# Taller edge steps for the last image, a PSUM read moved to ScalarE, and a new dealing-out of the last stages' steps

## The chip, the cores and the metric

The kernel runs on one NeuronCore of a Trainium2 chip. The metric is the device time of one execution in microseconds (us), lower is better. Five engines run in parallel, each with its own queue of instructions in order: TensorE (PE in the profile; its weight loads are PEld), VectorE (DVE), ScalarE (ACT), GpSimd (POOL) and SyncE (SP, which here only issues DMAs). They wait for each other through semaphores. ScalarE issues DMAs too, and those issues stand in the same queue as its computations.

## The reference, cut to what matters

Everything is float32. Layer 0 is an attention layer with linear attention over 64x64 pixels and 512 channels for 4 images; it ends in `y = BN(conv1x1(out)) + x`. Layer 1 works on that y, and most of the change lies in it:

```python
sobel = jnp.sqrt(sobel_h ** 2 + sobel_v ** 2 + 1e-08)      # four 3x3 edge filters, per channel
lap   = jnp.abs(dwconv(x, K_LAP))
diag  = jnp.maximum(jnp.abs(dwconv(x, K_D1)), jnp.abs(dwconv(x, K_D2)))
grad  = jnp.sqrt(sobel ** 2 + lap ** 2 + 1e-08)
E = jnp.stack([sobel, lap, diag, grad])
y = jnp.einsum('kbchw,koc->kbohw', E, w_branch) + ...       # 4 branches, 512 -> 128 channels each
feat = jax.nn.gelu(y, approximate=False)
pooled = ef.mean(axis=(2, 3))                               # over the whole image
att = sigmoid(gelu(pooled @ w_att1.T + b) @ w_att2.T + b)   # one factor per channel
z = jnp.einsum('bchw,oc->bohw', ef * att, w_fuse) + b_fuse  # then layer norm over channels, gelu, + x
```

The mean over the image stands between the branches and the fusion: no pixel of an image can be fused before all its edges have been computed.

## The kernel before, in words

**Stages.** For each image the *front* (class `Group`, four groups of heads per image, lines 220 to 610) computes the attention. Three generators then carry an image to the end: `project_out` (y, 32 steps, each one `yps` bank of 16 matmul records and one VectorE pass), `edge_branches` (the edges) and `fuse_out` (attention factors, then the fusion `zps` and the layer norm). While the front of image b runs, `advance` deals out steps of the three generators of image b-1 by planned lengths, so the edges of images 0, 1 and 2 run amid front work on every engine. This part covers about 1200 to 4340 us for the edges. After the front of the last image only generators are left (from about 4340 us): the rest of image 2 and all of image 3.

**Edges (lines 667 to 757).** A step u covers 4 rows of the image. `edges(u, pair)` loads a window of 6 rows of two of the four channel chunks and makes four maps of them: 11 VectorE operations (lines 696 to 722) and 4 ScalarE operations (Square L709, Abs L713, Square L719, Sqrt L723). `branches(u, ks, maps)` then multiplies two of the four branches, 256 pixels each, into the two halves of one PSUM bank (tile `br`, L730), applies the gelu to each half on ScalarE (L737, with a running sum for the mean) and stores both (L742). Each of images 0 to 2 has 16 steps u and thus 32 calls of `branches`, 96 in all; the last image has 32 more. One fp32 product of the code is two records in the profile, so that a call is 8 products and 16 records on TensorE.

**Order.** `manual_schedule` keeps TensorE's instructions in the order in which the code states them. For the other engines a scheduler sets the order when the program is built. Semaphore waits are derived from the tiles that instructions share. PSUM tiles of tag `ps` (`br`, `zps`, `yps`, `proj` and others) rotate over four banks.

**ScalarE's queue in the front.** After each projection (`project`, L262) ScalarE copies the bank (L268), for queries also applies a relu (L273), and issues four DMAs (L277). The gelu of a `branches` call stands behind whatever of this came first, and behind a table load when the function set changes (Sqrt and Gelu need different tables).

**The end of the program (lines 930 to 960).** After half of the last image's `project_out` steps, each of the 64 steps of the last image's edges is followed by exactly one step of `rest`: the 16 remaining `project_out` steps, then image 2's `fuse_out`. What is left of them, and the last image's `fuse_out`, comes last. In `fuse_out`, ScalarE squares each `zps` bank (L810) and VectorE reads the same bank once more to make z (L812).

Of the kernel before, what the change touches and what calls it, by code (L numbers as in the profile page):

```python
# [8 lines left out]
F32 = mybir.dt.float32  # L9
AF = mybir.ActivationFunctionType  # L10
ALU = mybir.AluOpType
AX = mybir.AxisListType

B, C, H, W = 4, 512, 64, 64
N = H * W
P = 128
NCH = C // P
NG = 4
NJ = N // 512
WB = W + 2  # L20
# [45 lines left out]
SHARE_Y, SHARE_E, SHARE_F = 90.0, 450.0, 100.0  # L66

WAIT_Y, WAIT_E, WAIT_F = 32.0, 16.0, 26.0

LEFT_E = 14.0  # L70

# [12 lines left out]
def conv_seq_kernel(  # L84
    ctx: ExitStack, tc, x, wqkv, dpk, wtab, proj, projc, pwk, bn0, consts, vec, watt1, batt1, watt2, wbr, wfuse, out
):
    nc = tc.nc

    const = ctx.enter_context(tc.tile_pool(name="const", bufs=1))
    small = ctx.enter_context(tc.tile_pool(name="small", bufs=2))  # L90
# [15 lines left out]
    def ps_tile(name):  # L106
        return psum.tile([P, 512], F32, tag="ps", name=name)
# [8 lines left out]
    def rows(ap, width=W):  # L116
        return ap.rearrange("p (r c) -> p r c", c=width)
# [55 lines left out]
    fbias = const.tile([P, 4], F32, name="fbias")  # L173
# [43 lines left out]
    first = ExitStack()  # L217
# [449 lines left out]
    def edge_branches(b, efs, pool_sb, side):  # L667

        y = ys[b % 2]
        with ExitStack() as stack:  # L670
            pool = stack.enter_context(tc.tile_pool(name=f"E{b}", bufs=2, side=side, reuse_waits="tile"))
            wbr_sb = pool.tile([P, 4, NCH, P], F32, name="wbr_sb", bufs=1)
            nc.sync.dma_start(out=wbr_sb, in_=wbr)
            share = SHARE_E / (2 * NJ * 4)

            slot = (2, 0, 1, 3)
            run = WB * 4 - 2
            yield 0.0

            def edges(u, pair):  # L680

                win = pool.tile([P, 2, 6 * WB], F32, name="win", tag="win")
                nc.sync.dma_start(
                    out=win,
                    in_=y[2 * pair : 2 * pair + 2].rearrange("c p r w -> p c (r w)")[:, :, 4 * u * WB : (4 * u + 6) * WB],
                )
                above, mid, below = (win[:, :, n * WB : (n + 4) * WB] for n in range(3))
                maps = pool.tile([P, 4, 2, 4 * WB], F32, name="maps", tag="maps", bufs=3)
                flat = maps.rearrange("p k c x -> p (k c x)")
                lap, sobel, grad = (maps[:, n, :, 0:run] for n in (0, 2, 3))  # L690


                dv = pool.tile([P, 2, 2, 4 * WB], F32, name="dv", tag="dv", bufs=1)
                down, smooth = dv[:, 0], dv[:, 1]
                dvs = dv.rearrange("p k c x -> p (k c x)")
                nc.vector.tensor_sub(down, below, above)
                nc.vector.tensor_add(smooth, below, above)
                nc.vector.scalar_tensor_tensor(smooth, mid, 2.0, smooth, ALU.mult, ALU.add)

                half = 2 * 4 * WB
                nc.vector.tensor_sub(flat[:, half : 3 * half - 2], dvs[:, 2 : 2 * half], dvs[:, 0 : 2 * half - 2])  # L703

                nc.vector.tensor_add(lap, mid[:, :, 0:run], mid[:, :, 2 : run + 2])
                nc.vector.scalar_tensor_tensor(lap, mid[:, :, 1 : run + 1], -6.0, lap, ALU.mult, ALU.add)
                nc.vector.tensor_add(lap, lap, smooth[:, :, 1 : run + 1])
                lap2 = pool.tile([P, 2, run], F32, name="lap2", tag="lap2", bufs=1)
                nc.scalar.activation(lap2, lap, AF.Square)  # L709
                first, second = (  # L710
                    maps[:, n : n + 2].rearrange("p k c x -> p (k c) x")[:, :, 0:run] for n in (0, 2)
                )
                nc.scalar.activation(first, first, AF.Abs)  # L713


                sv = flat[:, 3 * half : 4 * half - 2]
                nc.vector.tensor_add(sv, dvs[:, 0 : half - 2], dvs[:, 2:half])
                nc.vector.scalar_tensor_tensor(sv, dvs[:, 1 : half - 1], 2.0, sv, ALU.mult, ALU.add)
                nc.scalar.activation(second, second, AF.Square)  # L719
                nc.vector.tensor_add(sobel, sobel, grad)  # L720

                nc.vector.scalar_tensor_tensor(grad, lap2, SOBEL_EPS, sobel, ALU.add, ALU.add)
                nc.scalar.activation(second, second, AF.Sqrt, bias=sobel_eps)  # L723
                return maps

            def branches(u, ks, maps):
                ps = ps_tile("br")
                for n, k in enumerate(ks):
                    for c in range(NCH):
                        nc.tensor.matmul(  # L730
                            rows(ps)[:, 4 * n : 4 * n + 4, :], lhsT=wbr_sb[:, k, c, :],
                            rhs=rows(maps[c // 2][:, slot[k], c % 2, :], WB)[:, :, 0:W],
                            start=(c == 0), stop=(c == NCH - 1),
                        )
                o = pool.tile([P, 2, 256], F32, name="ef_o", tag="ef_o")
                for n, k in enumerate(ks):
                    nc.scalar.activation(  # L737
                        o[:, n, :], ps[:, 256 * n : 256 * n + 256], AF.Gelu,
                        bias=shift1[:, k : k + 1], scale=scale1[:, k : k + 1], accum_out=pool_sb[:, k, u : u + 1],
                    )  # L740
                step = ks[1] - ks[0]
                nc.scalar.dma_start(  # L742
                    out=efs[u // 2][:, ks[0] : ks[1] + 1 : step, 256 * (u % 2) : 256 * (u % 2) + 256], in_=o
                )

            held = []
            for u in range(2 * NJ + 1):
                first = [edges(u, 0)] if u < 2 * NJ else []
                yield share if u else share + WAIT_E
                if held:  # L750
                    branches(u - 1, (1, 2), held)
                    yield share
                    branches(u - 1, (0, 3), held)
                    yield share
                if first:
                    held = first + [edges(u, 1)]
                    yield share if u else share + WAIT_E

    def fuse_out(b, efs, pool_sb, side):

        y = ys[b % 2]
        with ExitStack() as stack:
            pool = stack.enter_context(tc.tile_pool(name=f"F{b}", bufs=2, side=side, reuse_waits="tile"))
# [39 lines left out]
            share = SHARE_F / (NJ * 5)  # L803

            def fuse(c, ef, zs, total):
                ps = ps_tile("zps")
                for k in range(4):
                    nc.tensor.matmul(ps, lhsT=wf_sb[:, k, ts(c, P)], rhs=ef[k], start=(k == 0), stop=(k == 3))  # L808
                sq = total if c == 0 else pool.tile([P, 512], F32, name="sq", tag="sq", bufs=3)
                nc.scalar.activation(sq, ps, AF.Square, bias=fbias[:, c : c + 1])  # L810
                z = pool.tile([P, 512], F32, name="z", tag="z", bufs=6)
                nc.vector.tensor_scalar(z, ps, fbias[:, c : c + 1], None, ALU.add)  # L812
                zs.append(z)
                if c:
                    nc.gpsimd.tensor_add(total, total, sq)
# [46 lines left out]
    def stages(b, heads, cheads, folded, side="right"):  # L862

        efs = [dram.tile([P, 4, 512], F32, name=f"ef{j}") for j in range(NJ)]
        pool_sb = small.tile([P, 4, 2 * NJ], F32, name="pool_sb")
        return [
            project_out(b, heads, cheads, folded, side), edge_branches(b, efs, pool_sb, side),
            fuse_out(b, efs, pool_sb, side),
        ]
# [9 lines left out]
    behind, due = [], [0.0]  # L879
# [58 lines left out]


    projected, edged, fused = stages(last.b, last.heads, last.cheads, last.folded, "left")  # L940
    next(fused)
    next(edged)
    next(projected)
    while len(behind) > 1:
# [2 lines left out]
    next(behind[0])  # L947
    for _ in range(NCH * NJ // 2):
        next(projected)
    rest = [projected] + behind  # L950
    for n, _ in enumerate(edged):
        while rest and next(rest[0], None) is None:
            rest.pop(0)
    for stage in rest + [fused]:
        for _ in stage:
            pass

# [94 lines left out]
```

## Time and profile before

| | |
|---|---|
| median of 3 runs (range) | 5078.56 us (5077.92 to 5086.61) |
| the profiled execution's own time | 5063.71 us |
| span of its instructions | 5061.9 us |
| mean granted TensorE clock | 0.967 |
| 4340 to 4600 us: PE / DVE / ACT busy | 254.2 / 97.8 / 57.6 of 260 us |
| 4597 to 4907 us: PE / DVE / ACT / POOL busy | 233.8 / 276.7 / 229.9 / 94.9 of 310 us |
| 4910 to 5062 us: PE / DVE / ACT busy | 121.4 / 80.4 / 71.0 of 152 us |
| table loads of ScalarE from 4440 us on | 78, of 1283 ns each |

The profile lists an engine's busy time and, in its views of waits and groups, the idle time before an instruction with what ended it. "issue" means that nothing visible ended it. `ACTq` and `SPq` rows are DMA issues: the engine's sequencer is occupied, though the engine doesn't count as busy. The end of a matmul record is modelled: records that follow each other without a wait overlap slightly in the listing.

### The profile page before, as it was taken

The page shows a single profiled execution, that of the slowest core. Times are in us where ns is not written, and L with a number is a line of the kernel's source. Part 1 is how long each engine was busy: PE and PEld are TensorE (multiplying, and loading weights), DVE is VectorE, ACT ScalarE, POOL GpSimd, SP SyncE. Part 2 cuts the span into 40 slices and gives each one's busy share as a digit, 9 for nine tenths or more (in the row PEclk, how much of TensorE's full clock was granted, in tenths as well). Part 3 has the DMA queues.
Part 4 walks back from the last instruction along what each step waited for, and adds up shares of the span by engine and source line. Part 5 has one row for each costly group of instructions (what it writes and reads, how often), then busy time and mean ns, then how long its engine had stood idle before and what let it go on. Part 6 is the DMA issues. An engine that isn't in the chain of part 4 may idle for free. (4 is left out here: it accounts for less than half of the span.)

```text
span 5061.9 us, 107134 instructions
## 1 busy us (share of the span) xinstructions
PE 4702.0 (93%) x46362; PEld 2739.7 (54%) x46362; DVE 2124.7 (42%) x2960; ACT 1626.5 (32%) x2833; POOL 392.7 (8%) x291
## 2 busy tenths in 40 slices
PE   9999999999999999799899999899989898898777
PEld 5665654455666554454465655454456665445443
DVE  1222221116556433211455653431146557157965
ACT  2112111004444423200345442320024445035765
POOL 0000000000000013100000000310000000001335
PEclk9999999999999999899999999999999999999889
DMA  6444466666656565676555665657655553774425
GB/s 196 138 123 130 132 206 190 158 165 181 192 189 183 179 205 170 197 178 156 176 176 181 193 202 176 213 188 167 163 173 175 184 169 129 200 184 118 151 88 172
DMA packets 635945, 866.26 MB, mean 171 GB/s; under 512 B 324393, under 2 KB 395081, under 8 KB 617041
## 3 DMA queue, kind: packets, MB, share of 16 engines
q1 hardware_dynamic: 551504, 758.68, 51.8%
q10 hardware_dynamic: 83968, 100.74, 6.4%
q8 instruction: 364, 5.96, 0.5%
q14 instruction: 109, 0.88, 0.1%
HBM read 578.09 MB, written 213.98 MB: 156 GB/s over the span
## 5 line engine op out<-in xcount | busy, mean ns | idle before, releaser
L262 PE MATMUL proj<-xt,w_sb 128*128 128x512 f32 x2048 | 955.8, 610 | 52.9 <-DMA xt<-in_x 31.8
L655 PE MATMUL yps<-hd,fold_sb 128*128 128x512 f32 x2048 | 899.6, 596 | 9.7 <-DMA hd<-heads 8.7
L396 PE MATMUL cv<-inp,mat 32*32 32x512 f32 x20480 | 730.2, 597 | 35.4 <-issue 27.3
L262 PEld LDWEIGHTS proj<-xt,w_sb 128*128 128x128 f32 x2048 | 382.7, 194 | 523.3 <-issue 450.7
L655 PEld LDWEIGHTS yps<-hd,fold_sb 128*128 128x128 f32 x2048 | 384.9, 190 | 493.5 <-issue 445.3
L396 PEld LDWEIGHTS cv<-inp,mat 32*32 32x32 f32 x20480 | 420.3, 103 | 314.6 <-issue 154.2
L730 PE MATMUL br<-maps,wbr_sb 128*128 128x256 f32 x2048 | 495.0, 396 | 51.8 <-ACT maps L713 42.2
L808 PE MATMUL zps<-ef,wf_sb 128*128 128x512 f32 x1024 | 469.9, 610 | 53.5 <-DMA ef<-ef 19.0
L730 PEld LDWEIGHTS br<-maps,wbr_sb 128*128 128x128 f32 x2048 | 399.7, 198 | 165.9 <-issue 51.3
L284 PEld LDWEIGHTS val<-w_sb,xt 128*128 128x128 f32 x4096 | 470.2, 192 | 33.9 <-issue 26.1
L284 PE MATMUL val<-w_sb,xt 128*128 128x128 f32 x4096 | 484.9, 277 | 0.6 <-DVE vt L291 0.3
L660 DVE SCALAR_TENSOR_TENSOR yt<-yps,shift,xr 128x512 f32<-128x512 f32 x128 | 96.1, 750 | 871.8 <-PE yps L655 788.9
L268 ACT COPY strip<-proj 128x512 f32<-128x512 f32 x256 | 149.1, 582 | 928.5 <-PE proj L262 910.4
L451 PE MATMUL corr<-near,ckt 128*32 128x160 f32 x8192 | 333.6, 315 | 35.0 <-DMA near<-near 28.4
L808 PEld LDWEIGHTS zps<-ef,wf_sb 128*128 128x128 f32 x1024 | 196.1, 195 | 296.6 <-issue 235.6
L241 POOL TENSOR_TENSOR mat<-dp_sb 128x1280 f32<-128x1280 f32 x32 | 77.2, 2414 | 3464.5 <-PE cv L396 2951.0
L451 PEld LDWEIGHTS corr<-near,ckt 128*32 128x32 f32 x8192 | 256.9, 111 | 131.5 <-issue 73.1
L703 DVE TENSOR_TENSOR maps<-dv 128x1054 f32<-128x1054 f32 x128 | 162.6, 1271 | 366.9 <-PE br L730 366.9
L312 ACT ACTIVATE kt<-tr 128x512 f32<-128x512 f32 x128 | 75.8, 593 | 528.9 <-PE tr L310 345.9
L737 ACT ACTIVATE ef_o<-br,shift,scale 128x256 f32<-128x256 f32 x256 | 142.3, 559 | 283.5 <-PE br L730 251.9
L360 DVE RECIPROCAL rec<-rec 128x512 f32<-128x512 f32 x64 | 214.4, 3350 | 1.7
L812 DVE TENSOR_SCALAR z<-zps,fbias 128x512 f32<-128x512 f32 x128 | 94.9, 744 | 283.4 <-DMA out<-z 97.0
(125 smaller groups left out, 4135.7 us busy)
## 6 DMA issues: line engine op xcount, KB each, us to landing
xt<-in_x SPq DMA_DIRECT2D x316, 512.0 KB
near<-near SPq DMA_DIRECT2D x512, 264.0 KB
inp<-strip ACTq DMA_DIRECT2D x1024, 64.0 KB
win<-y SPq DMA_DIRECT2D x128, 396.0 KB
near<-vt SPq DMA_DIRECT2D x512, 66.0 KB
y<-yt SPq DMA_DIRECT2D x128, 264.0 KB
yr<-y SPq DMA_DIRECT2D x128, 264.0 KB
heads<-q SPq DMA_DIRECT2D x128, 256.0 KB
```

What stands on the lines that cost most here:

```text
L262: nc.tensor.matmul(ps, lhsT=self.w[t][:, c, :], rhs=xs[self.b, j][c], start=(c == 0), stop=(c == NCH - 1))
L268: nc.scalar.copy(s, ps)
L284: nc.tensor.matmul(ps[:, ts(c, P)], lhsT=xs[self.b, j][n][:, ts(c, P)], rhs=self.w[VALUE][:, n, :], start=(n == 0), stop=(n == NCH - 1),)
L360: nc.vector.reciprocal(rec, rec)
L396: nc.tensor.matmul(rows(banks[i])[32 * j : 32 * j + 32, :, c0:c1], lhsT=self.mat[t][q, j, (dx + 2) * 8 + 4 * b : (dx + 2) * 8 + 4 * b + 4, :],
L451: nc.tensor.matmul(self.banks[jj][32 * i : 32 * i + 32, 160 * b : 160 * b + 160], lhsT=self.held["c", i][:, at : at + 32], rhs=v[:, 4 * n ...
L655: nc.tensor.matmul(ps, lhsT=fold_sb[g // NG][:, g % NG, ts(c, P)], rhs=hd[g], start=(g == 0), stop=(g == 2 * NG - 1),)
L660: nc.vector.scalar_tensor_tensor(yt[:, :, 1 : W + 1], rows(ps), shift0[:, c : c + 1], rows(xr), ALU.add, ALU.add)
L703: nc.vector.tensor_sub(flat[:, half : 3 * half - 2], dvs[:, 2 : 2 * half], dvs[:, 0 : 2 * half - 2])
L730: nc.tensor.matmul(rows(ps)[:, 4 * n : 4 * n + 4, :], lhsT=wbr_sb[:, k, c, :], rhs=rows(maps[c // 2][:, slot[k], c % 2, :], WB)[:, :, 0:W] ...
L737: nc.scalar.activation(o[:, n, :], ps[:, 256 * n : 256 * n + 256], AF.Gelu, bias=shift1[:, k : k + 1], scale=scale1[:, k : k + 1], accum_o ...
L808: nc.tensor.matmul(ps, lhsT=wf_sb[:, k, ts(c, P)], rhs=ef[k], start=(k == 0), stop=(k == 3))
```

## The change

Four things change.

1. The edges of the last image (`side == "left"`) go in steps of 8 rows instead of 4: half as many instructions, each twice as long, and each branch fills a bank of its own (512 pixels).
2. For that, `branches` is rewritten for all images: a bank is taken when the next one is needed, and each branch's gelu now stands directly behind its own matmuls, ahead of the second branch's matmuls. For images 0 to 2 the two branches still share a bank.
3. In image 2's fusion, z is made by ScalarE (Identity with bias) instead of VectorE.
4. The steps of `rest` are dealt out by planned lengths (5.5 us for a step of `project_out`, 2.9 for one of `fuse_out`) against the planned length of the edges; three shares are kept for the steps that make the attention factors; the last `fuse_out` takes its memory and loads its weights when `project_out` has ended, not before; the edges' memory is given back at the very end.

```diff
-            share = SHARE_E / (2 * NJ * 4)
+            tall = 8 if side == "left" else 4
+            steps, wide = H // tall, tall * W
+            share = SHARE_E / (steps * 4)
...
             def branches(u, ks, maps):
-                ps = ps_tile("br")
+                o = pool.tile([P, 2, wide], F32, name="ef_o", tag="ef_o")
                 for n, k in enumerate(ks):
+                    if n * wide % 512 == 0:
+                        bank = ps_tile("br")
+                    ps = bank[:, n * wide % 512 : n * wide % 512 + wide]
                     for c in range(NCH):
                         nc.tensor.matmul(
-                            rows(ps)[:, 4 * n : 4 * n + 4, :], lhsT=wbr_sb[:, k, c, :],
+                            rows(ps), lhsT=wbr_sb[:, k, c, :],
                             rhs=rows(maps[c // 2][:, slot[k], c % 2, :], WB)[:, :, 0:W],
                             start=(c == 0), stop=(c == NCH - 1),
                         )
-                o = pool.tile([P, 2, 256], F32, name="ef_o", tag="ef_o")
-                for n, k in enumerate(ks):
                     nc.scalar.activation(
-                        o[:, n, :], ps[:, 256 * n : 256 * n + 256], AF.Gelu,
+                        o[:, n, :], ps, AF.Gelu,
                         bias=shift1[:, k : k + 1], scale=scale1[:, k : k + 1], accum_out=pool_sb[:, k, u : u + 1],
                     )
...
-                nc.vector.tensor_scalar(z, ps, fbias[:, c : c + 1], None, ALU.add)
+                if b == B - 2:
+                    nc.scalar.activation(z, ps, AF.Identity, bias=fbias[:, c : c + 1])
+                else:
+                    nc.vector.tensor_scalar(z, ps, fbias[:, c : c + 1], None, ALU.add)
...
-    rest = [projected] + behind
-    for n, _ in enumerate(edged):
-        while rest and next(rest[0], None) is None:
-            rest.pop(0)
-    for stage in rest + [fused]:
+    rest, spent, given = [projected] + behind, 0.0, 0.0
+    def fill():
+        nonlocal spent
+        while rest and spent < given:
+            spent += FILL_Y if rest[0] is projected else FILL_F
+            if next(rest[0], None) is None:
+                if rest.pop(0) is projected:
+                    next(fused)
+    for share in edged:
+        if not share:
+            break
+        given += share * REST / SHARE_E
+        fill()
+    for _ in range(3):
+        next(fused)
+        given += (16 * FILL_Y + 44 * FILL_F - REST) / 3
+        fill()
+    for stage in rest + [fused, edged]:
```

More of the change, by code (lines that the diff above doesn't have):

```diff
@@ L68 @@
 WAIT_Y, WAIT_E, WAIT_F = 32.0, 16.0, 26.0
+FILL_Y, FILL_F = 5.5, 2.9
+REST = 16 * FILL_Y + 40 * FILL_F
 LEFT_E = 14.0
@@ L673, in edge_branches @@
             nc.sync.dma_start(out=wbr_sb, in_=wbr)
-            share = SHARE_E / (2 * NJ * 4)
+            tall = 8 if side == "left" else 4
+            steps, wide = H // tall, tall * W
+            share = SHARE_E / (steps * 4)
             slot = (2, 0, 1, 3)
-            run = WB * 4 - 2
+            run = WB * tall - 2
             yield 0.0
             def edges(u, pair):
-                win = pool.tile([P, 2, 6 * WB], F32, name="win", tag="win")
+                win = pool.tile([P, 2, (tall + 2) * WB], F32, name="win", tag="win")
                 nc.sync.dma_start(
                     out=win,
-                    in_=y[2 * pair : 2 * pair + 2].rearrange("c p r w -> p c (r w)")[:, :, 4 * u * WB : (4 * u + 6) * WB],
-                )
-                above, mid, below = (win[:, :, n * WB : (n + 4) * WB] for n in range(3))
-                maps = pool.tile([P, 4, 2, 4 * WB], F32, name="maps", tag="maps", bufs=3)
+                    in_=y[2 * pair : 2 * pair + 2].rearrange("c p r w -> p c (r w)")[
+                        :, :, tall * u * WB : (tall * u + tall + 2) * WB
+                    ],
+                )
+                above, mid, below = (win[:, :, n * WB : (n + tall) * WB] for n in range(3))
+                maps = pool.tile([P, 4, 2, tall * WB], F32, name="maps", tag="maps", bufs=3)
                 flat = maps.rearrange("p k c x -> p (k c x)")
                 lap, sobel, grad = (maps[:, n, :, 0:run] for n in (0, 2, 3))
-                dv = pool.tile([P, 2, 2, 4 * WB], F32, name="dv", tag="dv", bufs=1)
+                dv = pool.tile([P, 2, 2, tall * WB], F32, name="dv", tag="dv", bufs=1)
                 down, smooth = dv[:, 0], dv[:, 1]
@@ L698, in edges @@
                 nc.vector.scalar_tensor_tensor(smooth, mid, 2.0, smooth, ALU.mult, ALU.add)
-                half = 2 * 4 * WB
+                half = 2 * tall * WB
                 nc.vector.tensor_sub(flat[:, half : 3 * half - 2], dvs[:, 2 : 2 * half], dvs[:, 0 : 2 * half - 2])
@@ L734, in branches @@
                         )
-                o = pool.tile([P, 2, 256], F32, name="ef_o", tag="ef_o")
-                for n, k in enumerate(ks):
                     nc.scalar.activation(
-                        o[:, n, :], ps[:, 256 * n : 256 * n + 256], AF.Gelu,
+                        o[:, n, :], ps, AF.Gelu,
                         bias=shift1[:, k : k + 1], scale=scale1[:, k : k + 1], accum_out=pool_sb[:, k, u : u + 1],
                     )
[L741 to L744, printed above, removed]
+                at, step = wide * u % 512, ks[1] - ks[0]
+                nc.scalar.dma_start(out=efs[wide * u // 512][:, ks[0] : ks[1] + 1 : step, at : at + wide], in_=o)
             held = []
-            for u in range(2 * NJ + 1):
-                first = [edges(u, 0)] if u < 2 * NJ else []
+            for u in range(steps + 1):
+                first = [edges(u, 0)] if u < steps else []
                 yield share if u else share + WAIT_E
@@ L757, in edge_branches @@
                     yield share if u else share + WAIT_E
+            yield 0.0
     def fuse_out(b, efs, pool_sb, side):
@@ L864, in stages @@
         efs = [dram.tile([P, 4, 512], F32, name=f"ef{j}") for j in range(NJ)]
-        pool_sb = small.tile([P, 4, 2 * NJ], F32, name="pool_sb")
+        pool_sb = small.tile([P, 4, 2 * NJ if side == "right" else NJ], F32, name="pool_sb")
         return [
@@ L940, in conv_seq_kernel @@
     projected, edged, fused = stages(last.b, last.heads, last.cheads, last.folded, "left")
-    next(fused)
     next(edged)
```

## The prediction, made before the changed kernel was run

> **What bounds the kernel now.** I read the page's first part, then the busy time by stage, then single calls of `branches` in the timeline, then the groups of the late stage.
>
> ```profile
> PE 4702.0 (93%) x46362; PEld 2739.7 (54%) x46362; DVE 2124.7 (42%) x2960; ACT 1626.5 (32%) x2833; POOL 392.7 (8%) x291
> ```
>
> ```profile
> 1200.00:1790.00 590.00, 562.09 (x6911) 368.69 (x6910) 322.92 (x486) 273.98 (x500) 11.97 (x5) 0.98 0.61 190
> 2490.00:3080.00 590.00, 565.22 (x7178) 377.77 (x7177) 323.52 (x491) 267.08 (x476) 12.46 (x5) 0.98 0.61 191
> 3770.00:4340.00 570.00, 513.13 (x6546) 336.09 (x6542) 327.24 (x484) 255.34 (x445) 7.48 (x7) 0.95 0.54 169
> 4597.00:4907.00 310.00, 233.81 (x679) 141.27 (x679) 276.68 (x328) 229.93 (x317) 94.90 (x56) 0.87 0.40 125
> ```
>
> Columns of the second, after the length of the stretch: busy PE, PEld, DVE, ACT, POOL, then the granted clock. In the three stretches that hold the edges of images 0, 1 and 2, TensorE is busy 1640 of 1750 us: it is the bound, and what stops it costs time. From 4597 to 4907 us, the edges of the last image beside image 2's fusion, VectorE is busy 277 of 310 us, and TensorE waits there: VectorE is the bound. So the change's taller edges, z and dealing-out lie in these 310 us; its rewritten `branches` lies in the 1750 as well.
>
> **What the skill says.** "PSUM — Partial Sum Buffer", section "PSUM bank collisions raise a hardware error": two engines may not touch one bank and quadrant at once, and the scheduler orders them whatever halves they use. The program before never had to, since both branches were multiplied before any gelu; no trace shows it yet. "TensorE: Matmul & The Clock Gate", section "Step-by-step: what each phase is for": matmuls stay in program order, so a waiting one holds all behind it; and its "Part 1: The HAM clock gate": idle TensorE falls to half clock for a window of 3.4 us. The trace agrees on the second:
>
> ```profile
> 3883.40:3886.80 3.40, 0.11 (x4) 0.11 (x4) 3.40 (x2) 1.31 (x2) 0.00 (x0) 0.99 0.65 148
> 3886.80:3890.20 3.40, 3.40 (x45) 1.83 (x46) 3.40 (x7) 1.17 (x1) 0.00 (x0) 0.51 0.17 46
> ```
>
> After a gap of 3.47 us the next 3.4 us ran at 0.51. Of the gaps of 2.5 to 3.5 us in this trace 17 of 18 were followed so, of those of 1.5 to 2.5 us 7 of 19. "SBUF — State Buffer", section "SBUF: two separate sides": VectorE, with two SBUF inputs, and GpSimd share a port pair that one holds at a time. L717 took 0.70 us in a quiet stretch and 872 ns in the mean from 4597 to 4907 us, where GpSimd runs: it agrees.
>
> **Part 1: gelu ahead of the second branch, images 0 to 2.** The order of the built programs shows TensorE's first 22,901 instructions unchanged, but in all 96 calls the first matmul of the second branch now waits for the first branch's gelu. Queued behind it: the rest of the call and every later projection and convolution. The price of one call comes from the timeline:
>
> ```profile
> 1570.33 3.62 PE L730 MATMUL br<-maps,wbr_sb 128*128 128x256 f32 x16
> 1573.88 2.55 PE L451 MATMUL corr<-near,ckt 128*32 128x160 f32 x64
> 1570.53 0.58 ACT L268 COPY strip<-proj 128x512 f32<-128x512 f32 x1 [2.38 <-PE proj L262]
> 1571.15 2.41 ACTq L277 DMA_DIRECT2D inp<-strip  x4
> 1573.59 1.28 ACT L737 ACT_TABLE_LOAD   x1 [2.48 <-issue]
> 1574.89 0.56 ACT L737 ACTIVATE ef_o<-br,shift,scale 128x256 f32<-128x256 f32 x1
> 1575.35 0.20 ACT L737 ACTIVATION_READ_ACCUMULATOR ef_o<-br,shift,scale 128x1 f32 x1
> ```
>
> The eighth of the 16 records ends near 1572.2. The gelu can't start before 1574.89: ScalarE first copies a projection, issues four DMAs, loads a table. It ends, with its accumulator, at 1575.55; a released matmul starts some 0.05 us later (in this trace L713 ended at 4603.08 and L730 started at 4603.13). So TensorE will stand from 1572.2 to 1575.6: 3.4 us, where before it went on. An idle ScalarE would give the least: 0.04 us to start, 0.56, 0.10, 0.05, or 0.75 us.
>
> I did this for all 96 calls, with ScalarE's queue (copies, DMA issues, table loads) as in the trace; the order of ScalarE's instructions around the call is the same in 85 of the 96. Visible gaps: 33 calls at the least 0.75 us, 24.7 us; 13 up to 1.5 us, 12.8; 21 up to 2.5 us, 43.5; 19 up to 4 us, 61.2; 10 above, 51.5. Sum 193.7 us. To it:
>
> - Records without a wait overlap by some 0.17 us in the listing (a group of 16 takes 3.62 us, the next starts 3.45 after it), and a restarted group takes 0.1 us longer (1.13 against 1.03 for four records): 96 x 0.27 = 26 us.
> - Half clock: 29 gaps above 2.5 us at 90% and 21 of 1.5 to 2.5 us at 37%, each losing half of 3.41 us: 44 + 13 = 57 us, of which I take 45, as small matmuls are bound by weight loads too.
> - Given back: TensorE idles 106 us in the three stretches (28, 25 and 53). Gaps within 14 us after a call come to 18 us, within 30 us to 42; a later TensorE finds these waits shorter. I take -30.
>
> Together +235 us. Bounds: from below ScalarE never has a backlog, 96 x (0.75 + 0.27) = 98, less 42 given back, about +55; from above 194 + 26 + 57 - 5, about +270. A gain is excluded, since nothing is removed from TensorE here.
>
> **Part 2: edges of 8 rows.** VectorE: in the quiet timeline a 528-wide operation follows the last after 0.615 us and the 1054-wide L703 takes 1.17 us, so that 526 elements cost about 0.56 us and the fixed part is about 0.05 us. 16 x 11 = 176 instructions go for the whole image; of the 23 steps at work in the 310 us, half, 126 instructions, 6 us. ScalarE: 0.632 us for 524 and 1.07 for 1048 elements leave 0.2 us fixed: 46 instructions fewer in the window, 9 us. The program has 51 loads of tables for Sqrt and Gelu before, 27 after; in the window some 18 x 1.283 = 23 us go. Gelus: 25 pairs of 0.559 become one of 0.77 (estimate from the slope): 9 us. TensorE: 128x256 and 128x512 records go at the same rate (0.215 and 0.43 us), so nothing.
>
> **Part 3: z on ScalarE.** VectorE loses 32 x 0.740 us:
>
> ```profile
> L812 DVE TENSOR_SCALAR z<-zps,fbias 128x512 f32<-128x512 f32 x32 | 23.5, 740 | 12.1 <-ACT total L810 10.5 <-DMA out<-z 1.5
> L810 ACT ACTIVATE sq<-zps,fbias 128x512 f32<-128x512 f32 x24 | 16.1, 675 | 8.2 <-PE zps L808 7.7 <-ACT ef_o L737 0.5
> L730 PE MATMUL br<-maps,wbr_sb 128*128 128x256 f32 x386 | 109.7, 443 | 48.1 <-ACT maps L713 42.2 <-DVE z L812 5.1 <-ACT maps L723 0.7
> ```
>
> ScalarE gains 32 x 0.675 = 22 us (priced as L810, same bank and size). Edge operations and the next gelus queue behind it; TensorE gets each `zps` bank back only after both readings by ScalarE.
>
> **Part 4: dealing out.** 12 four-row calls' worth of branches instead of 9 now come before the last `yps`. That moves 3 x 3.45 = 10 us of matmuls into a stretch where TensorE is full (+10 us), and with them about 3 x 7.3 x 1.27 = 28 us of VectorE and 17 us of ScalarE work out of the 310 us. The order after shows image 2's fusion used up before the last edges, so the attention factors still lie bare; the last step's chain is twice as tall: I take +6 us. The fusion's weights (three DMAs on SP's queue) now queue where `project_out` ends, ahead of later windows; 250 us of edges cover them, about 3 us if not. POOL gets nothing.
>
> Sum for the 310 us: VectorE 277 - 6 - 23 - 28 = 220; ScalarE 230 + 22 - 9 - 23 - 9 - 17 = 194; TensorE 234 - 10 = 224. VectorE's share of the stretch was 277 of 310; with the same looseness 220 becomes 246, a gain of 64. Less 10, 6 and 3: **-45 us**. Bounds: -75 if the stretch closes to its engines; +5 if ScalarE's chains make it looser (1.3 times 220 is 286).
>
> **Sum.** Against the profiled execution, span 5061.9 and time 5063.71 us: +235 - 45 = +190, 5253.7 us. It lies 14.9 us below the median of the runs, 5078.56, to which I add the same: **5268.6 us**.
>
> **The rivals.**
> - *ScalarE without backlog.* TensorE's stops let ScalarE drain, and every call costs the least: 98, no half clock, 20 given back: +78 - 45 = +33, 5111 us. For it: ScalarE is busy only 46% of the stretches. Against: the copies, DMA issues and table load stand directly ahead of the gelu, produced by the projection just before. 13%.
> - *The waits are swallowed.* Faster: the stops take the place of TensorE's idle 106 us, so that the calls cost nearly nothing, and the tail's -45 remains: 5034 us. It decides if a call costs below 0.47 us (45 / 96). Against: only 18 to 42 us of idle lie near the calls. 4%.
> - *ScalarE becomes the late bound.* Part 1 as forecast, no tail gain: 5314 us. 13%.
> - *Forecast.* 70%.
>
> **How the numbers follow.** The measurement tells 0.2%, about 10 us, from no change. The likeliest case gives 5268.6, with part 1 from 180 to 265 and the tail from -65 to -15: 5194 to 5329. The range reaches down towards the first rival, 5150, and up to 5335. Faster 0.04 (swallowed), same 0.03 (between that and the first rival), slower 0.93.
>
> **What would show it.** A wait of TensorE `br` on ScalarE `ef_o`, absent from the groups of before in these stretches, about 96 times and near 190 us; the last edge stretch shortened to about 250 us with VectorE no longer 90% busy; fewer table loads by 24. Wrong if that wait is below 100 us, if clock and projections stay as they were, or if the late stretch doesn't shrink.

## The result and the profile after

The changed kernel takes 5304.25 us (median of 4 runs, 5303.24 to 5309.46) against 5078.24 us before: ratio 1.0441, 95% interval 1.0424 to 1.0457, or +226 us where +190 was forecast. The profiled execution took 5303.73 us with a span of 5301.9, 240 us more than that of before. First part of its page, then its busy time by stretch (length; PE, PEld, DVE, ACT, POOL; clock); the first three stretches run from the first to the last `br` matmul of images 0, 1 and 2, the fourth is B of the table below:

```profile
PE 4769.4 (90%) x46106; PEld 2710.2 (51%) x46106; DVE 2092.2 (39%) x2752; ACT 1604.7 (30%) x2713; POOL 394.5 (7%) x291
```

```profile
1208.90:1868.10 659.20, 567.59 (x6776) 366.00 (x6774) 319.20 (x479) 278.20 (x498) 11.97 (x5) 0.95 0.52 162
2593.20:3266.40 673.20, 577.09 (x7018) 377.13 (x7017) 322.28 (x487) 270.73 (x472) 12.44 (x5) 0.95 0.52 162
3974.40:4607.90 633.50, 532.72 (x6504) 338.46 (x6502) 321.14 (x475) 256.97 (x441) 7.40 (x7) 0.93 0.47 146
4868.52:5144.77 276.25, 222.19 (x481) 94.62 (x479) 215.53 (x145) 184.12 (x215) 92.19 (x54) 0.90 0.41 130
```

The same four stretches before:

```profile
1204.20:1775.90 571.70, 543.79 (x6776) 357.20 (x6774) 318.59 (x479) 271.59 (x494) 11.97 (x5) 0.98 0.60 187
2497.60:3071.40 573.80, 549.01 (x7018) 367.82 (x7017) 321.87 (x487) 263.61 (x468) 12.46 (x5) 0.98 0.60 188
3777.20:4336.20 559.00, 505.91 (x6504) 330.89 (x6502) 323.31 (x477) 252.49 (x439) 7.48 (x7) 0.95 0.53 167
4593.98:4905.14 311.16, 236.54 (x688) 143.63 (x687) 277.60 (x328) 228.73 (x313) 94.90 (x56) 0.87 0.40 125
```

TensorE ran exactly as many records in the first three as before (6776, 7018, 6504) and took longer for them. The lines of the view of waits over these images, costliest first (us in total, times, longest):

```profile
PE br L741 <- ACT ef_o L746: 180.5, 96, 6.4
PE proj L265 <- DMA xt<-in_x: 31.1, 3, 22.4
PE cv L399 <- issue: 28.6, 21, 2.7
```

The first line did not exist before: 96 stops for 96 calls. The others did, at much the same size. The call that the prediction worked out (1570.33 us there) now looks so:

```profile
1637.99 1.89 PE L741 MATMUL br<-maps,wbr_sb 128*128 128x256 f32 x8
1643.25 2.79 PE L741 MATMUL br<-maps,wbr_sb 128*128 128x256 f32 x8 [3.37 <-ACT ef_o L746]
1638.19 0.58 ACT L271 COPY strip<-proj 128x512 f32<-128x512 f32 x1 [2.38 <-PE proj L265]
1638.80 2.42 ACTq L280 DMA_DIRECT2D inp<-strip  x4
1641.25 1.28 ACT L746 ACT_TABLE_LOAD   x1 [2.48 <-issue]
1642.55 0.56 ACT L746 ACTIVATE ef_o<-br,shift,scale 128x256 f32<-128x256 f32 x1
1643.01 0.19 ACT L746 ACTIVATION_READ_ACCUMULATOR ef_o<-br,shift,scale 128x1 f32 x1
```

The 16 records have become 8 and 8, with 3.37 us between them (3.4 was worked out), in which ScalarE does what it did before: copy, four DMA issues, table load, gelu. The second eight take 2.79 us instead of 1.89; the granted clock was 0.66 from 1643.2 to 1646.6 us.

By stretch, in us (length, and in brackets TensorE's idle time and what the clock took, that is the time weighted with the part not granted):

| stretch | before | after | difference |
|---|---|---|---|
| edges of image 0 | 571.7 (27.9; 11.9) | 659.2 (91.6; 32.4) | +87.5 |
| edges of image 1 | 573.8 (24.8; 11.9) | 673.2 (96.1; 34.1) | +99.4 |
| edges of image 2 | 559.0 (53.1; 27.3) | 633.5 (100.8; 46.1) | +74.5 |
| start and the two stretches between | 2631.7 | 2641.9 | +10.2 |
| from there to the last projection (A) | 257.8 | 260.6 | +2.8 |
| to the last edge matmul (B) | 311.2 | 276.2 | -35.0 |
| to the end (C) | 156.8 | 157.2 | +0.4 |

The images' edges lost 261.4 us; the late part (A, B, C) gained 31.8. ScalarE's table loads fell from 211 to 187, by the 24 that the prediction named.

### The profile page after: what moved, and what is told of

Read it like the earlier page. It is cut to its first block, busy times and chain, and to the rows that moved or that the text cites. A ratio compares the mean times of both kernels' runs of the same rounds, so it can differ in the third digit from the quotient of the medians.

```text
span 5301.9 us, 106106 instructions
## 1 busy us (share of the span) xinstructions
PE 4769.4 (90%) x46106; PEld 2710.2 (51%) x46106; DVE 2092.2 (39%) x2752; ACT 1604.7 (30%) x2713; POOL 394.5 (7%) x291
## 5 line engine op out<-in xcount | busy, mean ns | idle before, releaser
L741 PE MATMUL br<-maps,wbr_sb 128*128 128x256 f32 (+1 forms) x1792 | 542.8, 452 | 199.0 <-ACT ef_o L746 181.4
L741 PEld LDWEIGHTS br<-maps,wbr_sb 128*128 128x128 f32 x1792 | 357.3, 207 | 386.5 <-ACT ef_o L746 221.4
L816 PEld LDWEIGHTS zps<-ef,wf_sb 128*128 128x128 f32 x1024 | 196.4, 195 | 305.3 <-issue 246.8
L711 DVE TENSOR_TENSOR maps<-dv 128x1054 f32<-128x1054 f32 (+1 forms) x112 | 159.8, 1427 | 445.0 <-PE br L741 444.9
L746 ACT ACTIVATE ef_o<-br,shift,scale 128x256 f32<-128x256 f32 (+1 forms) x224 | 133.2, 595 | 433.3 <-PE br L741 390.5
L412 ACT ACTIVATE co<-cv 128x256 f32<-128x256 f32 x256 | 93.8, 397 | 339.1 <-PE cv L399 339.1
## 6 DMA issues: line engine op xcount, KB each, us to landing
near<-near SPq DMA_DIRECT2D x512, 264.0 KB
y<-yt SPq DMA_DIRECT2D x128, 264.0 KB
yr<-y SPq DMA_DIRECT2D x128, 264.0 KB
```

The source lines that it names most:

```text
L741: nc.tensor.matmul(rows(ps), lhsT=wbr_sb[:, k, c, :], rhs=rows(maps[c // 2][:, slot[k], c % 2, :], WB)[:, :, 0:W], start=(c == 0), stop=(c ...
L746: nc.scalar.activation(o[:, n, :], ps, AF.Gelu, bias=shift1[:, k : k + 1], scale=scale1[:, k : k + 1], accum_out=pool_sb[:, k, u : u + 1],)
```

## Experiments

Ratios are against the kernel before on the same chip, whose median there was 5051 to 5062 us; lengths of stretches are from each run's profile. The diffs show the lines that matter; `...` stands for what was left out.

**1. The branches mended, all else changed.** Images 0 to 2 only; `parts` holds the `ps` of both branches:

```diff
                     for c in range(NCH):
                         nc.tensor.matmul(...)
+                    if tall == 4:
+                        continue
                     nc.scalar.activation(o[:, n, :], ps, AF.Gelu, ...)
+                for n, k in enumerate(ks):
+                    if tall == 8:
+                        break
+                    nc.scalar.activation(o[:, n, :], parts[n], AF.Gelu, ...)
```

> The changed kernel with one thing undone: for images 0 to 2 both branches are multiplied before either gelu, as in the kernel before; everything for the last images stays changed. Theory (the three image stages lost 261 us to the waits for the first gelu, and the late part alone gained 32): about 5304 - 261 = 5043 us, 0.993 of the kernel before, with no wait of TensorE's second branch on the gelu and granted clock back near 0.967. Rival (the loss comes from how the changed program orders the other engines, or from the late part): stays above 5200 us.

Measured 5025.91 us, ratio 0.9933 (0.9916 to 0.9951). The three stretches take 566.1, 575.1 and 562.8 us, together 1704.0 against 1704.5 before and 1965.9 changed; the wait is gone. All of the loss is in this one ordering, and the rest of the change is a gain of 0.7%, with 1 outside its interval. The longest waits left in these images are of other kinds:

```profile
PE corr L454 <- DMA near<-near: 29.5, 7, 9.2
```

**2. The gelus' new place alone, in the kernel before.**

```diff
                 for n, k in enumerate(ks):
+                    ps = bank[:, 256 * n : 256 * n + 256]
                     for c in range(NCH):
                         nc.tensor.matmul(...)
+                    if side == "right":
+                        nc.scalar.activation(o[:, n, :], ps, AF.Gelu, ...)
                 for n, k in enumerate(ks):
+                    if side == "right":
+                        break
                     nc.scalar.activation(o[:, n, :], bank[:, 256 * n : 256 * n + 256], AF.Gelu, ...)
```

> The kernel before with one thing changed: for images 0 to 2 each gelu stands directly behind its own branch's matmuls, in the shared bank. Theory: 5078 + 261 = about 5339 us, 1.051 of before, with a wait of br on ef_o of about 180 us in 96 places and some 60 us more of lost clock. Rival (the loss needs the other parts of the change): below 5150 us.

Measured 5317.38 us, ratio 1.0503 (1.0476 to 1.0531); the three stretches together 1979.2 us, +274.7. It needs nothing else of the change.

```profile
PE br L732 <- ACT ef_o L738: 181.7, 96, 6.3
PE br L732 <- ACT maps L713: 41.2, 8, 11.4
```

**3. The gelus' new place, but a bank for each branch.**

```diff
-                    if n * wide % 512 == 0:
-                        bank = ps_tile("br")
-                    ps = bank[:, n * wide % 512 : n * wide % 512 + wide]
+                    ps = ps_tile("br")[:, 0:wide]
```

> The changed kernel with the gelus where the change put them, but each branch of images 0 to 2 in a PSUM bank of its own. Theory (the wait comes from the shared bank, not from the place of the gelu): the wait for the same call's gelu is gone; the calls take two of the four rotating banks, so that some calls wait for a gelu of an earlier call; I put these at 10 to 60 us, which gives 5055 to 5105 us. Rival (the place of the gelu in ScalarE's queue costs, whatever the bank): stays within 30 us of 5304.

Measured 5033.78 us, ratio 0.995 (0.9932 to 0.9968); stretches 1707.0 us. Its longest waits in these images are no gelus:

```profile
PE corr L454 <- DMA near<-near: 27.9, 7, 8.8
PE proj L265 <- DMA xt<-in_x: 24.4, 3, 17.7
PE den L369 <- ACT rq L276: 21.9, 11, 7.5
```

So it is the sharing that makes the wait, not the place of the gelu in ScalarE's queue. The halves that a matmul writes and a gelu reads never overlap; what they share is the bank, and also the tile, from which the semaphore waits are derived. Experiment 3 gives each branch a bank and a tile of its own, so the runs don't tell which of the two makes the program wait. The cost of taking two of four rotating banks, 10 to 60 us in the expectation, was too high: no wait for a gelu above 0.15 us is left in these images, and the ratio's interval overlaps that of experiment 1.

**4. The DMAs behind each projection issued by GpSimd, with and without the waits.**

```diff
-                nc.scalar.dma_start(out=inps[t][r::4, n, b : b + 8, :], ...)
+                nc.gpsimd.dma_start(out=inps[t][r::4, n, b : b + 8, :], ...)
```

In the changed kernel:

> The changed kernel with the four DMAs behind each projection issued by GpSimd instead of ScalarE, so that they no longer stand ahead of the gelu. Theory (the size of a stop is what ScalarE's queue holds ahead of the gelu): taking 0.6 us per DMA out of the gaps of the changed kernel's trace leaves about 107 of 180 us of visible wait, and with fewer stops above 2.5 us the clock loses some 30 us less: about 5304 - 73 - 30 = 5200 us, if GpSimd's issues are in time. Rival (a stop is a fixed price of a handshake between the two engines, whatever is queued): the wait stays near 180 us and the time near 5304.

Measured 5087.11 us, ratio 1.0056 (1.0034 to 1.0078). The wait shrank as expected to

```profile
PE br L741 <- ACT ef_o L746: 122.8, 97, 5.7
```

(107 worked out), but the whole fell by twice the expected 104 us. The three stretches with edges lost 140 us, 92 of TensorE's idle time (59 of it the wait) and 48 of its busy time, where the clock had been put at 30; and the stretches without edges, which have no such waits, lost 81: the two between the images went from 1433 to 1368 us. So moving the DMAs does more than shorten the stops, and only the same kernel without the stops tells the two apart.

> The last run's kernel (the DMAs behind each projection issued by GpSimd) with both branches of images 0 to 2 multiplied before either gelu: its partner without the waits. Theory: with the DMAs out of ScalarE's queue the order of gelu and matmul costs about the 122 us of visible wait that the partner showed, with little lost clock; 5087 - 125 = about 4962 us, 0.980 of before. Rival (the partner's waits were taken from idle time that it would have had anyway): above 5030 us.

Measured 4932.46 us, ratio 0.9744 (0.9722 to 0.9766). Between the two the three stretches differ by 159.7 us (1826.1 and 1666.4), of which 112.0 are idle time of TensorE, 22.2 clock (the time weighted with the part not granted), 15.7 the overlap that the listing hides (96 x 0.163 us: records without a wait start that much before the listed end of the one ahead) and some 10 the restarts (96 x 0.105). These are the same stops, smaller, because less stood in ScalarE's queue. "About 122 us with little lost clock" left out the overlap, the restarts and the clock.

**5. Half of the calls.** The gelu stays ahead only in the calls for branches (0, 3); against experiment 1:

```diff
-                    if tall == 4:
+                    if tall == 4 and ks[0] == 1:
                         continue
                     nc.scalar.activation(o[:, n, :], ps, AF.Gelu, ...)
                 for n, k in enumerate(ks):
-                    if tall == 8:
+                    if tall == 8 or ks[0] == 0:
                         break
                     nc.scalar.activation(o[:, n, :], parts[n], AF.Gelu, ...)
```

> The changed kernel in which only half of the 96 calls keep the gelu ahead of the second branch: those for sobel and grad, branches (0, 3); the calls for branches (1, 2) multiply first. In the changed kernel's trace these 48 calls held 60 us of the visible wait, with 2 stops above 2.5 us, the other 48 held 121 us with 23 such stops. Theory (a stop costs what ScalarE has queued, and long stops cost clock on top): 60 us of wait, 8 of overlap and some 8 to 13 of clock, about 78 us above the kernel with both mended (0.9933 of before), 1.009 of before. Rival (each call costs the same): half of 262 us, 1.019.

Measured 5097.82 us, ratio 1.0089 (1.0065 to 1.0113), with

```profile
PE br L743 <- ACT ef_o L750: 61.4, 49, 3.2
```

The rival's 1.019 lies outside the interval: calls don't cost the same. Together with experiment 4 this fits a price that is set by what ScalarE has queued in that place.

**6. The late part taken apart.** z alone in the kernel before:

```diff
-                nc.vector.tensor_scalar(z, ps, fbias[:, c : c + 1], None, ALU.add)
+                if b == B - 2:
+                    nc.scalar.activation(z, ps, AF.Identity, bias=fbias[:, c : c + 1])
+                else:
+                    nc.vector.tensor_scalar(z, ps, fbias[:, c : c + 1], None, ALU.add)
```

> The kernel before with only z of image 2's fusion made by ScalarE. Theory (VectorE bounds the last edges' stretch, and z is 24 of its 277 us): the stretch from the last projection to the last edge matmul, 311 us before, gets some 15 to 25 us shorter, 0.996 of before. Rival (ScalarE's queue, which then reads each bank twice, holds TensorE as long): no change, within 5 us.

Measured 5051.11 us, ratio 0.9984 (0.9976 to 0.9992); stretch B 308.1 us, 3 shorter. The rival holds for B: z took 23.7 us of VectorE there, VectorE is busy 10 us less (267.5), and B lost 3. A is 5 us shorter too, but no z of image 2 lies in it, and A took 250.1 us in experiment 2, whose late code is that of before.

The mended kernel of experiment 1 with z left on VectorE:

```diff
-                if b == B - 2:
-                    nc.scalar.activation(z, ps, AF.Identity, bias=fbias[:, c : c + 1])
-                else:
-                    nc.vector.tensor_scalar(z, ps, fbias[:, c : c + 1], None, ALU.add)
+                nc.vector.tensor_scalar(z, ps, fbias[:, c : c + 1], None, ALU.add)
```

> The changed kernel with the order of the branches mended (5026 us on its chip, late stretch 278 us) and z of image 2 left on VectorE. If z carries its share of the late gain: the late stretch is 15 to 25 us longer, about 295 us. Rival (after the taller edges ScalarE's chain is what ends last, so z on ScalarE gives nothing): within 5 us of 278, or shorter.

Measured 5015.41 us, ratio 0.9911 (0.9893 to 0.9929); B 264.0 us. The rival is right, and more: beside taller edges z on ScalarE costs 14 us. B takes 276.1 to 278.6 us in the six profiles with this late code and z on ScalarE, and 264.0 in both with z on VectorE (experiment 7 has the other).

The mended kernel with 4-row edges:

```diff
-            tall = 8 if side == "left" else 4
+            tall = 4
...
-        pool_sb = small.tile([P, 4, 2 * NJ if side == "right" else NJ], F32, name="pool_sb")
+        pool_sb = small.tile([P, 4, 2 * NJ], F32, name="pool_sb")
```

> The changed kernel with the order of the branches mended and the last image's edges in steps of 4 rows again (z on ScalarE, steps dealt out by length). If the taller steps give what I worked out (6 us of VectorE, 41 us of ScalarE, but a twice as tall last chain): the late stretch is 5 to 15 us longer than 278 us. Rival (the tall steps make the stretch looser, and the gain is all from z and the dealing-out): shorter than 278 us by more than 5.

Measured 5030.91 us, ratio 0.9943 (0.9925 to 0.9961); B 274.5 us, C 160.6. Neither expectation: with z on ScalarE the tall edges change B and C together by 1 us.

The dealing-out alone, the mended kernel with both of the last two edits:

```diff
-            tall = 8 if side == "left" else 4
+            tall = 4
...
-                if b == B - 2:
-                    nc.scalar.activation(z, ps, AF.Identity, bias=fbias[:, c : c + 1])
-                else:
-                    nc.vector.tensor_scalar(z, ps, fbias[:, c : c + 1], None, ALU.add)
+                nc.vector.tensor_scalar(z, ps, fbias[:, c : c + 1], None, ALU.add)
```

> Of the late part only the new dealing-out and the later start of the last fusion: edges of 4 rows, z on VectorE, branches multiplied first. Theory (the dealing-out carries most of the late gain): late stretch between the last projection and the last edge matmul, 311 us before, 265 to 280 us. Rival (it takes the taller edges to gain): above 295 us.

Measured 5031.26 us, ratio 0.9954 (0.994 to 0.9968); B 272.5, C 162.6 us. In one table, A + B + C:

| late part | A | B | C | sum |
|---|---|---|---|---|
| before | 257.8 | 311.2 | 156.8 | 725.8 |
| z only | 252.8 | 308.1 | 156.7 | 717.6 |
| dealing-out only | 259.7 | 272.5 | 162.6 | 694.8 |
| dealing-out, z | 260.5 | 274.5 | 160.6 | 695.6 |
| dealing-out, tall edges | 260.3 | 264.0 | 155.6 | 679.9 |
| all three (experiment 1) | 259.7 | 278.0 | 155.9 | 693.6 |

The dealing-out gives 31 us, the tall edges 15 more, and z on ScalarE takes 14 of these back. A alone differs by up to 8 us between profiles of one late code, so these sums are no finer than that; B and C without A give 33, 15 and 14. What the dealing-out removes in B is TensorE's wait for the edges, before and then with the dealing-out alone:

```profile
PE br L730 <- ACT maps L713: 42.2, 8, 11.4
```

```profile
PE br L743 <- DVE z L831: 19.0, 3, 9.3
PE zps L827 <- DVE z L831: 15.1, 3, 7.6
PE att_ps L810 <- ACT hid L806: 8.2, 1, 8.2
PE br L743 <- ACT maps L721: 6.5, 2, 5.3
```

Against that, TensorE's waits for z rise from 17 to 34 us; the clock takes 12 us less (41 and 29), and 8 us of TensorE's work has moved ahead of B. Which part of the dealing-out does this (the planned lengths, the shares kept for the attention factors, the later start of the last fusion) no run separates. The busy times of B for the last row and the row above it (experiment 1, then with z on VectorE):

```profile
4594.15:4872.14 277.99, 223.79 (x480) 95.15 (x479) 215.53 (x145) 184.00 (x215) 92.11 (x54) 0.88 0.40 130
```

```profile
4598.32:4862.30 263.98, 217.11 (x481) 93.44 (x479) 229.83 (x177) 165.38 (x183) 88.60 (x54) 0.91 0.42 136
```

VectorE has 14 us less to do with z on ScalarE, and the stretch is 14 us longer: no engine's sum bounds it. The waits in B of the changed kernel, and the view of z's line there, point to what does:

```profile
PE br L741 <- ACT z L821: 13.9, 2, 7.6
PE zps L816 <- ACT z L821: 11.9, 4, 7.9
PE zps L816 <- DVE wf_sb L805: 10.4, 1, 10.4
PE var L830 <- ACT z L821: 9.3, 3, 6.3
PE var L830 <- POOL total L826: 7.0, 2, 6.1
```

```profile
L821 ACT ACTIVATE z<-zps,fbias x32: 667/680/695, 4902.0 to 5129.1; 128x512 f32<-128x512 f32 x32
...
  DMA out<-z: 9.5, 7
```

35 us of TensorE's 54 us of idle time end with z on ScalarE, which itself stood 9.5 us until a store of an older z had landed. With z on VectorE the waits for z come to 20:

```profile
PE br L743 <- DVE z L831: 8.3, 1, 8.3
PE var L838 <- DVE z L831: 6.4, 2, 4.8
PE zps L827 <- DVE z L831: 5.7, 3, 3.3
```

Against experiment 1 (whose waits for z come to 35 us too) half of the 14 us is idle time of TensorE (54.2 to 46.9 us), the other half is busy time, with less of the clock lost (0.88 to 0.91). That z on ScalarE holds banks for longer fits this, but isn't shown: with 4-row edges TensorE waits 34 us for z on VectorE and 25 for z on ScalarE, and B is 2 us longer with the latter.

**7. The best of it.** The second kernel of experiment 4 with z on VectorE; against experiment 1:

```diff
-                nc.scalar.dma_start(out=inps[t][r::4, n, b : b + 8, :], ...)
+                nc.gpsimd.dma_start(out=inps[t][r::4, n, b : b + 8, :], ...)
...
-                if b == B - 2:
-                    nc.scalar.activation(z, ps, AF.Identity, bias=fbias[:, c : c + 1])
-                else:
-                    nc.vector.tensor_scalar(z, ps, fbias[:, c : c + 1], None, ALU.add)
+                nc.vector.tensor_scalar(z, ps, fbias[:, c : c + 1], None, ALU.add)
```

> What the runs point to: 8-row edges and new dealing-out, z of image 2 on VectorE, branches multiplied before the gelus, and the DMAs behind each projection issued by GpSimd. If the gains add: 0.9744 less (0.9933 - 0.9911) = 0.972 of before. If z on VectorE meets GpSimd's DMA issues on their shared port, no better than 0.9744; there are no such issues in the late stretch, so I expect 0.972.

Measured 4914.2 us, ratio 0.9726 (0.9705 to 0.9747): 2.7% faster than before. Its B is 264.0 us, as without GpSimd's DMAs, so the gain of z on VectorE is there; the intervals of this ratio and 0.9744 overlap.

## Why the prediction was right

**Part 1, forecast +235, measured +261.** Mechanism and place held: TensorE's second branch waits for the first one's gelu in the shared bank, 96 times, where TensorE is the bound. Its terms:

- Visible gaps: 193.7 forecast, 180.5 measured. At the least value there were 43 calls, not 33; ScalarE had now and then caught up, as the first rival had it, but by 13 us in all, where that rival needed 122 (193.7 - 96 x 0.75).
- Overlap and restart: 26 forecast, 26 measured. The gaps counted from start to start come to 196.4 us, 15.9 above the visible; of a restarted call the first two records stand 0.32 us apart instead of 0.215, 10 us in 96 calls. The prediction misread the line that it gives for the overlap (the next group starts 3.55 us after the start of the call, not 3.45), but between two records of a call the overlap is 0.16, as taken.
- Half clock: 45 taken of 57 worked out, about 53 measured. The time weighted with the part not granted rose by 61.4 us (51.2 to 112.6), but some of that lay in the stops themselves. TensorE runs the same records in the same order here, so that the times from start to start can be subtracted one by one: records that ran at half clock took 49 us more, restarted records some 4. A discount was due, a smaller one.
- Given back: 30 forecast, nothing measured. TensorE's idle time other than before `br` was 102.1 us before and 104.3 after. This is the step of the sum that failed most: the idle time near a call was not waiting for something that the stop let catch up.

With these the sum closes: 180.5 + 26 + 53 + 2 = 261.5 of 261.4 us. The forecast of +235 was nearer than its terms, since 13 us too much in the gaps made up for a third of the 40 us that clock and idle time were short.

**The swallowed waits** (4%) would have needed these 102 us to shrink. They did not.

**Parts 2 to 4, forecast -45, measured -32.** The busy times forecast for the 310 us came out: VectorE 220 forecast and 215.5 measured, ScalarE 194 and 184.1, TensorE 224 and 222.2. For VectorE this is partly luck: the dealing-out took 25 us of its work out of B (28 forecast), but the tall edges took 22 instead of 6, since more of the edge work now lies ahead of B, and z took 14 instead of 23. The step "with the same looseness 220 becomes 246" failed: the stretch is 276 us, 1.28 times VectorE's time instead of 1.12. The upper bound that the text gave for it (1.3 times) is where it went, though ScalarE isn't the bound by its sum: TensorE waits 35 us for z on ScalarE there, a cost that part 3 names and puts no number to. Of the parts, z was counted as 23 us of VectorE; alone it gave 3 in B (8 by the medians, 0.9976 to 0.9992 of before), and beside tall edges it took 14. The dealing-out carries the whole, 31 us. The +10 us for A was +2.8. The +6 for the last chain isn't seen: C is 157.2 against 156.8, and with the new dealing-out tall edges make it 5 to 7 us shorter.

**Sum.** +261 - 32 and +10 in the stretches without edges make the 240 us between the profiles. Such stretches take 2622 to 2637 us in the other runs with ScalarE's DMAs, and 2642 here, so most of the 10 us is scatter. The medians differ by 226. By its number alone the result, 5304 us, would fit the rival "ScalarE becomes the late bound" (5314) better than the forecast (5269); the stretches decide against that rival, since the late part did gain 32 us and part 1 cost 26 more than forecast.

What stays open: why GpSimd as issuer helps as much as it does outside the edges (1424 to 1365 us in the stretches between, experiment 1 against its partner). TensorE's waits for `xt` loads fell from 30.5 to 12.8 us over the whole kernel, those for `rq` from 27.0 to 19.8, and the clock took 22 instead of 48 us in these stretches; no run separates these. Open too is whether the program waits for the bank or for the tile, and why z on ScalarE costs what it does.

## What to carry to other kernels

Two halves of a PSUM bank that are one tile were one resource here: the matmul of the second half waited until the reader of the first was done. So finish all matmuls of a bank before its first reader, or give each reader its own bank. Price such a wait by what stands in the reader's queue just there (copies, DMA issues, table loads), add the clock that the gap costs, and don't credit idle time elsewhere unless it waits for the same engine. Moving work off the fullest engine is no gain by itself: look at what the other engines wait for before and after; here z cost 14 us more where VectorE had 14 us less to do.

## What the runs showed of the hardware that was not expected

A DMA issued by ScalarE holds its queue for 0.6 us (four in 2.42 us), and issued by GpSimd it took that out of the gelus' way: the wait fell from 181.4 to 122.8 us, and the mended kernel from 0.9933 to 0.9744, while GpSimd's busy time rose from 393 to 937 us and VectorE's stayed (2093 and 2089 us). The clock dropped less surely after a gap than the trace of before suggested, and after shorter ones: counted as in the prediction, half clock followed 27 of 34 gaps of 2.5 to 4 us in the changed kernel (22 of 23 before), and 11 of 24 of 2 to 2.5 us.
